# A Mamba layer on one core: GpSimd's operations in one written order, softplus by a timetable, a second DMA sum, and the residual added one chunk later

## The chip, the cores and the metric

The kernel runs on one core of a Trainium2 chip. The time is device microseconds (us) of one execution. Before the change, three runs took 2245.73, 2246.95 and 2251.04 us; the median is 2246.95 us. The engines have these short names in the profile: PE (TensorE, matrix products and transposes, which write to PSUM), ACT (ScalarE), DVE (VectorE), POOL (GpSimd) and SP (SyncE, which only issues DMAs here). Each works through its own queue in order. What a reader of one engine's result waits for is a semaphore.

## What is computed

The network has four layers; the change touches the first alone, two Mamba blocks m1 and m2 one behind the other on 2048 tokens (2 images of 1024 tokens) of 256 channels. Of the reference, cut to what matters:

```python
xs, res = jnp.split(u @ in_w + in_b, 2, axis=-1)       # 512 channels each
xs = silu(causal_conv4(xs) + conv_b)
dt, Bm, Cm = jnp.split(xs @ xproj_w, ...)               # 16 | 16 | 16
delta = softplus(dt @ dt_w + dt_b)
dA  = exp(delta[..., None] * A)                         # 16 states
dBu = delta[..., None] * Bm[:, :, None, :] * xs[..., None]
hst = dA_t * hst + dBu_t                                # over the tokens of an image
y_t = einsum('bdn,bn->bd', hst, C_t)
out = ((y + xs * Dp) * silu(res)) @ out_w + out_b       # then layer norm, and x is added
```

For each of the 16 states n there is a recurrence over the tokens for 512 channels, and y is a sum over n.

## The kernel before

**Units.** A block's tokens are cut into chunks of 512, so that there are eight units: m1's chunks 0 to 3, then m2's. `layer0` (from L662) lets three units overlap: while the scan of unit u runs, the back of unit u-1 (gate, silu, y, output projection, norm, residual) and the front of unit u+1 (convolution, x-projection, softplus) run in its gaps, and the entering projection of unit u+2.

**The scan of a unit** (`scan`, L461) goes over n = 0 to 15. For one n:
- POOL makes two products h = du * b of 128x1024 elements (L513). Their tile has six buffers, so POOL can lead by three n.
- ACT makes four decays da = exp(A delta) in PSUM (L525, three buffers).
- DVE runs four scans of 128x512 over them, in place in h (L529).
- PE transposes h in 16 pieces into PSUM tiles ht (L486, three buffers).
- The four tiles are weighted by C and summed into ya: by DVE, which adds in place (L501), or for some n by ACT, which only writes (L499).

ACT writes five of the 16 n: n = 0 into ya itself, n = 2 (`ASIDE`) into a second sum yb, and n = 4, 7 and 10 (`ADDED`) into a scratch tile `tail`, from which a DMA that POOL issues (L520) adds them into yb, `LATER` = 3 states on. At n = 3 of the next unit another such DMA adds yb into ya. yb and `tail` have one buffer each; ya has two.

**Softplus of the next unit** is done in two halves of 256 channels in `front`: PE's projection m_dt (L428), ACT's |.| and relu (L433, L437), exp (L440), ln (L442), then (e + 1) - 1 in two ACT steps on du (L448, L450), and on POOL sub, add, add to delta, and the product du = delta * x (L451, L453, L455, L457). Both halves use the same e and ln tiles.

**The back of a unit** (`back`) ends with the output projection into two PSUM tiles m_out_0 and m_out_2, the layer norm of their rows (`norm_rows`: statistics and `ln_off` on DVE, L176 to L184; `ln_rs` and the normalised rows `m_tail<-m_out` on ACT, L186), transposes back (mm_t, L197), ACT's scale and bias into `tail` (L627), and POOL's additions to x (L630; m2 adds its input x as well).

**PSUM.** The pool `ps_mm` (L674) has two buffers. The projections m_in, m_conv, m_dt, m_g, m_y, m_out and mm_t, and the tap products of layer 1 (w1t, taps_ps), all take their tiles from it.

**What sets the order.** The steps of these helpers are generators. `paced(63, steps)` spreads them over the 63 gaps ("slots") of a unit's scan: slot s comes after scan s + 1, so that n is about (s + 1) / 4. A tuple (g, many, first, end) gives `many` steps of g the slots from `first` up to `end`. That order of writing is only a priority: the framework's scheduler then decides, by dependences and free buffers, in which order each engine's instructions stand in its queue. The slots that matter here:

```python
            steps += [(f, Mamba.STEPS, 35, 63) for f in fronts]     # softplus, 18 steps
            steps += [(b, 4, 36, 50) for b in done]                 # output projection
            steps += [(e, Mamba.ENTER, 44, 62) for e in enters]     # entering projection
            steps += [(b, 3, 54, 62) for b in done]                 # norm, 2 x residual
```

A helper `behind` lets m2's diagonal tap matrices (POOL) follow the scan's products; for all else POOL's order is the scheduler's.

Of the kernel before, what the change touches and what calls it, by code (L numbers as in the profile page):

```python
# [66 lines left out]
class Net:  # L67


    def __init__(self, ctx, tc, cols, rows):  # L70
        self.tc, self.nc = tc, tc.nc
        nc = self.nc
        const = ctx.enter_context(tc.tile_pool(name="const", bufs=1))
        self.gates = []
# [82 lines left out]
    def functions(self, which, *after):  # L157

        with ExitStack() as order:
# [7 lines left out]
            )  # L167

    def norm_rows(self, outs, ins, by=None):

# [81 lines left out]
class Mamba:  # L252

    ASIDE = 2
    ADDED = 4, 7, 10
    LATER = 3
    ENTER = 4
    HEAD = 12  # L260
    STEPS = 18

    def __init__(self, net, m, pools, xt, x, in_w, out_w, xproj_w, dt_w):
        self.net, self.m, self.xt, self.x = net, m, xt, x
        self.wpool, self.one, self.two, self.scanp, self.dram, self.ps_mm, self.ps_da, self.ps_ht = pools
        self.weights = in_w, out_w, xproj_w, dt_w
        self.chunks = {}
        self.carry = None
        self.due, self.pre = {}, {}
# [19 lines left out]
    def diagonals(self):  # L289

        self.taps = self.wpool.tile(
            [P, NDC * 4, P], F32, tag="taps", name=f"{self.m}_taps"
        )
        for i in range(NDC * 4):
            self.net.nc.gpsimd.tensor_scalar_mul(
                self.taps[:, i, :], self.net.ident, self.net.col(f"{self.m}_conv_w", i)
            )
            yield

    def load_rest(self):  # L300
# [10 lines left out]
        for dc in range(NDC):  # L311
            nc.gpsimd.tensor_scalar_mul(self.skip[:, dc, :], net.ident, net.col(f"{m}_D", dc))
        yield
# [5 lines left out]
    def enter(self, j):  # L319

        net, nc, m, one = self.net, self.net.nc, self.m, self.one
        tok = slice(j * TC, (j + 1) * TC)
        pre = one.tile([P, NDC, 3 + TC], F32, tag="pre", name=f"{m}_pre_{j}")
        self.pre[j] = pre
        if self.first(j):
            nc.gpsimd.memset(pre[:, :, 0:3], 0.0)
        else:
            nc.gpsimd.tensor_copy(pre[:, :, 0:3], self.carry)
        for mc in range(NDC):
            ps = self.ps_mm.tile([P, TC], F32, tag="mm", name=f"{m}_in_{j}_{mc}")  # L330
            for kc in range(NCC):
                nc.tensor.matmul(  # L332
                    ps, lhsT=self.in_sb[:, kc, mc * P : (mc + 1) * P], rhs=self.xt[:, kc, tok],
                    start=(kc == 0), stop=(kc == NCC - 1),
                )
            nc.scalar.activation(pre[:, mc, 3:], ps, AF.Identity, bias=net.col(f"{m}_in_b", mc))
            if mc == NDC - 1 and not self.first(j + 1):
                self.carry = self.wpool.tile(
                    [P, NDC, 3], F32, tag="carry", name=f"{m}_carry_{j}", bufs=2
                )  # L340
                nc.gpsimd.tensor_copy(self.carry, pre[:, :, TC : TC + 3])
            yield

    def front(self, j, alone=False):
# [73 lines left out]
        else:  # L418
            parts = [slice(0, 2), slice(2, NDC)]
        for a in parts:  # L420
            if not alone:
                eb, lb = free[:, :2], free[:, 2:]
            else:
                eb, lb = e[:, a], ln[:, a]
            for k, dc in enumerate(range(a.start, a.stop)):
# [10 lines left out]
                else:  # L436
                    nc.scalar.activation(delta[:, dc, :], ps, AF.Relu, bias=b)  # L437
                yield
            with net.tc.issue_after(net.loaded.ins):
# [4 lines left out]
            w = du[:, a, :]  # L444
            if alone:
                nc.vector.tensor_scalar(w, eb, 1.0, -1.0, ALU.add, ALU.add)
            else:
                nc.scalar.activation(w, eb, AF.Identity, bias=net.one)  # L448
                yield
                nc.scalar.activation(w, w, AF.Identity, bias=net.minus_one)  # L450
            eng.tensor_sub(w, eb, w)  # L451
            yield
            eng.tensor_add(lb, lb, w)  # L453
            yield
            eng.tensor_add(delta[:, a, :], delta[:, a, :], lb)  # L455
            yield
            eng.tensor_mul(w, delta[:, a, :], xs[:, a, :])  # L457
            yield
        self.chunks[j] = xs, bd, ct, delta, du

    def scan(self, j, before, between, start=False, last=False):  # L461
# [18 lines left out]
        def rest(n, hs):  # L480


            for i in range(TPC):
# [23 lines left out]
        for n in range(NS):  # L507
# [3 lines left out]
            for g in range(NDC // G):  # L511
                h = scanp.tile(half, F32, tag="h", name=f"{m}_h_{j}_{n}_{g}", bufs=6)
                made = (nc.vector if start and n == 0 else nc.gpsimd).tensor_mul(  # L513
                    h, du[:, g * G : (g + 1) * G, :], b.unsqueeze(1).to_broadcast(half)
                )
                hs.append(h)
            self.product = made
# [20 lines left out]
        for _ in between:  # L538
            pass
        self.due = {} if last else {self.LATER: (ya, yb)}  # L540
        return before
# [5 lines left out]
    def back(self, j, last=False, joined=True):  # L547
# [24 lines left out]
        if last:  # L572
            tail = self.tail(f"{m}_tail_{j}")
            for cc in range(NCC):
                x = tail[:, (2 + cc) * TC : (3 + cc) * TC]
                at = j % (HW // TC) * TC
                nc.sync.dma_start(x, self.x[j // (HW // TC), cc, :, at : at + TC])
                nc.gpsimd.tensor_scalar_add(x, x, net.col(f"{m}_ln_b", cc))
                nc.gpsimd.tensor_add(xt[:, cc, tok], xt[:, cc, tok], x)
                yield  # L580
# [36 lines left out]
        for cc in range(NCC):  # L617
# [11 lines left out]
            )  # L629
            nc.gpsimd.tensor_add(xt[:, cc, tok], xt[:, cc, tok], r)  # L630
            if self.x is not None:
                x = tail[:, (3 - cc) * TC : (4 - cc) * TC]
                at = j % (HW // TC) * TC
                nc.sync.dma_start(x, self.x[j // (HW // TC), cc, :, at : at + TC])
                nc.gpsimd.tensor_add(xt[:, cc, tok], xt[:, cc, tok], x)
            yield
# [25 lines left out]
def layer0(net, x, x_dram, m1, m2, load_image, taps, conv_dram, lg):  # L662
# [5 lines left out]
    with (  # L668
# [27 lines left out]

        def behind(m, steps):

            while True:
                with tc.issue_after(m.product.ins):  # L700
                    if next(steps, steps) is steps:
                        return
                yield
# [5 lines left out]
        before, done = iter(()), []  # L709
        aside = taps.make(ps_mm, conv_dram)  # L710
        for u, (m, j) in enumerate(units):
            joined = u + 1 < len(units)
            steps = [(b, NDC, 4, 20) for b in done]
            if u:
# [16 lines left out]
            if u == NCH - 2:  # L731

                steps.append((behind(m, blocks[1].diagonals()), NDC * 4, 24, 40))
# [43 lines left out]
        for _ in islice(done[0], 2):  # L777
            pass
        acc = {2: taps.bank(ps_ht.tile([P, TC], F32, tag="ht", name="early_acc2"))}
        both(taps.convolve(0, pair, acc), done[0], 3)  # L780
# [1085 lines left out]
```

## Time and profile before

One execution was profiled. It took 2244.33 us, of which the trace spans 2242.6 us; the two differ by 1.7 us, and the median of the three runs is 2.6 us (0.12%) above it.

| what | us |
|---|---|
| profiled execution / its span | 2244.33 / 2242.6 |
| first scan starts | 51.7 |
| units 0 to 7, from first scan to first scan of the next | 107.3, 119.4, 138.7, 137.1, 138.4, 139.3, 146.2, 157 (to the last scan) |
| end of layer 0 | about 1169 |
| DVE busy in a unit 1 to 7 | 110.7 to 112.3 |
| mean granted clock of PE, whole span | 0.905 |

A page of the profile gives for a group of equal instructions the source line, the engine, out<-in by the names in the program, the count, the total and the mean time, and the idle time of that engine just ahead of them with what ended it. The waits are the same idle times sorted by who waited for whom ("us in total, times, longest us"). A timeline lists instructions with start and duration; in square brackets stands the idle time before one and what released it. A table of windows gives the busy time of each engine in stretches of the span, with the count of instructions, the granted PE clock, the share of DMA time and GB/s.

### The profile page before, as it was taken

To read this page: it belongs to the slowest core of one execution; us is meant where nothing else is said; L and a number is where in the kernel's file an instruction comes from. 1 tells how busy PE (TensorE), PEld (TensorE's weight loads), DVE (VectorE), ACT (ScalarE), POOL (GpSimd) and SP (SyncE) were. 2 spreads that over 40 slices of the span, in tenths; PEclk is the share of its full clock that TensorE was granted. 3 is DMA by queue.
4 is the path that set the end of the run, shared out by engine and by line. 5 is a ranking of instruction groups with operands and counts; after the bars stand their busy time and mean duration, and the time that the engine had idled before them with its cause. 6 is when DMAs were issued, how large, how long until landed. Compare 5 with 4: busy or idle time off the path is not lost.

```text
span 2242.6 us, 26709 instructions
## 1 busy us (share of the span) xinstructions
PE 1880.2 (84%) x9428; PEld 1306.9 (58%) x9428; DVE 1357.8 (61%) x2086; ACT 924.6 (41%) x1658; POOL 1042.8 (47%) x701
## 2 busy tenths in 40 slices
PE   7788778687787876879999989958999599949996
PEld 3454445444454553545565645637999467649994
DVE  6998959689696895978543285762222444442223
ACT  4777667566675665756321253321111122211111
POOL 3897679676786668875432350003333100023331
PEclk9889789797897978979999999978999799969997
DMA  2243323233232322442121000007999300059997
GB/s 104 67 106 78 78 72 75 66 76 81 70 93 58 87 63 56 103 91 67 30 47 20 29 33 0 19 19 267 329 330 337 138 1 20 17 180 320 332 326 284
DMA packets 94959, 256.33 MB, mean 114 GB/s; under 512 B 35963, under 2 KB 52224, under 8 KB 80228
## 3 DMA queue, kind: packets, MB, share of 16 engines
q1 hardware_dynamic: 77636, 198.29, 26.5%
q0 software_dynamic: 12192, 51.66, 9.8%
q10 hardware_dynamic: 4992, 4.59, 0.6%
q8 instruction: 79, 1.29, 0.3%
q14 instruction: 60, 0.49, 0.1%
HBM read 204.60 MB, written 19.37 MB: 100 GB/s over the span
## 4 chain that ended last, share of the span: by engine, by line
PE 32%; issue 6%; DVE 4%; DMA 4%; POOL 4%; ACT 1%; POOLq 0%; ACTq 0%; DVEq 0%
PE h L1673 6%; PE acc L883 3%; PE o L1687 3%; PE av L1397 3%; PE h L1220 2%; PE sc L1371 2%; DMA l_yd<-y,target 2%; POOL x L1643 2%; POOL l_yd L1693 2%; PE w L1229 1%; PE early_acc L883 1%; DMA x<-l_zd,source 1%; PE mm_t L197 1%; PE kvp L1129 1%; PE o L1042 1%
## 5 line engine op out<-in xcount | busy, mean ns | idle before, releaser
L513 POOL TENSOR_TENSOR m_h<-m_du,m_b 128x1024 f32<-128x1024 f32 x254 | 598.1, 2412 | 219.5 <-PE m_ht L486 95.7
L486 PE MATMUL m_ht<-ident,m_h 128*128 128x128 f32 x2048 | 369.4, 308 | 216.3 <-DVE m_ya L501 92.8
L486 PEld LDWEIGHTS m_ht<-ident,m_h 128*128 128x128 f32 x2048 | 263.3, 156 | 412.3 <-DVE m_h L529 145.8
L525 ACT ACTIVATE m_da<-m_delta,m_aneg 128x512 f32<-128x512 f32 x512 | 349.1, 691 | 254.3 <-DVE m_h L529 226.5
L529 DVE TENSOR_TENSOR_SCAN m_h<-m_da,m_state,m_h 128x512 f32<-128x512 f32 x256 | 316.7, 1267 | 70.9 <-POOL m_h L513 45.3
L1643 POOL DMA_INDIRECT x<-l_zd,source x82 | 84.0, 1025 | 578.1 <-issue 222.3
L529 DVE TENSOR_TENSOR_SCAN m_h<-m_da,m_h 128x512 f32<-128x512 f32 x256 | 301.0, 1205 | 69.7 <-POOL m_h L513 39.6
L1673 PEld LDWEIGHTS h<-xts,we 128*128 128x128 f32 x2528 | 297.3, 194 | 7.6 <-issue 3.9
L1673 PE MATMUL h<-xts,we 128*128 128x128 f32 x2528 | 298.5, 277 | 2.5 <-issue 1.9
L501 DVE SCALAR_TENSOR_TENSOR m_ya<-m_ht,m_ct,m_ya 128x512 f32<-128x512 f32 x352 | 253.0, 730 | 55.4 <-PE m_ht L486 54.8
L1679 ACT ACTIVATE hid<-h 128x512 f32<-128x512 f32 x79 | 47.2, 597 | 415.1 <-PE h L1673 415.1
L1680 DVE TENSOR_TENSOR hid<-hid,h 128x512 f32<-128x512 f32 x79 | 54.3, 687 | 266.6 <-PE h L1673 266.6
L1687 PE MATMUL o<-we,hid 128*128 128x256 f32 x632 | 150.6, 380 | 3.9 <-DVE hid L1680 2.3
L1693 POOL DMA_INDIRECT l_yd<-y,target x79 | 79.1, 1001 | 135.9 <-DVE y L1692 132.3
L367 PE MATMUL m_conv<-m_pre,m_taps 128*128 128x512 f32 x240 | 123.0, 639 | 1.4 <-ACT m_tail L627 1.1
L1687 PEld LDWEIGHTS o<-we,hid 128*128 128x128 f32 x632 | 113.7, 190 | 17.8 <-DVE hid L1680 3.0
L883 PE MATMUL early_acc<-x,early 128*98 128x448 f32 (+24 forms) x308 | 101.1, 455 | 0.4 <-DVE lg L900 0.4
L883 PE MATMUL acc<-x,pair 128*98 128x416 f32 (+21 forms) x308 | 92.8, 450 | 0.0
L332 PE MATMUL m_in<-x,m_in_sb 128*128 128x512 f32 x128 | 74.5, 715 | 2.6 <-DVE x L247 1.3
L1692 DVE COPY y<-o 128x256 f32<-128x256 f32 x79 | 33.5, 424 | 70.0 <-PE o L1687 69.8
L557 PE MATMUL m_g<-x,m_gate_sb 128*128 128x512 f32 x128 | 70.3, 664 | 5.1 <-ACT m_tail L186 4.5
L451 POOL TENSOR_TENSOR m_du<-m_e,m_du 128x1024 f32<-128x1024 f32 x14 | 33.2, 2372 | 83.8 <-ACT m_du L450 83.8
(319 smaller groups left out, 2787.1 us busy)
## 6 DMA issues: line engine op xcount, KB each, us to landing
we<-in_l_experts_dram SPq DMA_DIRECT2D x82, 1536.0 KB, 9.3
m_b<-m_bd SPq DMA_DIRECT2D x128, 256.0 KB, 3.3
m_yb<-m_s POOLq DMA_DIRECT2D x24, 1024.0 KB, 8.5
m_ya<-m_yb POOLq DMA_DIRECT2D x7, 1024.0 KB, 8.6
w<-in_l_w_dram SPq DMA_DIRECT2D x21, 256.0 KB, 2.7
l_zd<-l_z SPq DMA_DIRECT2D x7, 512.0 KB, 2.9
l_yl<-l_yd SPq DMA_DIRECT2D x10, 256.0 KB, 5.1
l_yl<-l_yd ACTq DMA_DIRECT2D x10, 256.0 KB, 5.9
```

The source lines that it names most:

```text
L332: nc.tensor.matmul(ps, lhsT=self.in_sb[:, kc, mc * P : (mc + 1) * P], rhs=self.xt[:, kc, tok], start=(kc == 0), stop=(kc == NCC - 1),)
L367: nc.tensor.matmul(ps, lhsT=self.taps[:, dc * 4 + k, :], rhs=pre[:, dc, k : k + TC], start=(k == 0), stop=(k == 3),)
L486: nc.tensor.transpose(ps[:, dc * P : (dc + 1) * P], hs[dc // G][:, dc % G, i * P : (i + 1) * P], net.ident,)
L501: nc.vector.scalar_tensor_tensor(ya[:, i, :], ps, c, ya[:, i, :], ALU.mult, ALU.add)
L513: made = (nc.vector if start and n == 0 else nc.gpsimd).tensor_mul(h, du[:, g * G : (g + 1) * G, :], b.unsqueeze(1).to_broadcast(half))
L525: net.decayed = nc.scalar.activation(da, delta[:, dc, :], AF.Exp, scale=self.aneg[:, i : i + 1])
L529: nc.vector.tensor_tensor_scan(h, da, h, 0.0 if first else state[:, n, dc : dc + 1], ALU.mult, ALU.add)
L883: nc.tensor.matmul(a[:, lo - 16 * k : hi - 16 * k, co : co + n], lhsT=lhsT, rhs=self.x[:, kc, b, lo - r0 : hi - r0, ci : ci + n], start=(u ...
L1643: nc.gpsimd.indirect_dma_start(out=x, out_offset=None, in_=zd[:, :], in_offset=bass.IndirectOffsetOnAxis(ap=source[:, g : g + 1], axis=0), ...
L1673: nc.tensor.matmul(ps[:, at], lhsT=w12[:, s, kc, at], rhs=xt[:, kc * P : (kc + 1) * P], start=(kc == 0), stop=(kc == NCC - 1),)
L1687: nc.tensor.matmul(ps[:, :C], lhsT=ht[:, mc * P : (mc + 1) * P], rhs=w[:, 8 + mc, :], start=(mc == 0), stop=(mc == NHC - 1),)
L1693: nc.gpsimd.indirect_dma_start(out=yd[g], out_offset=bass.IndirectOffsetOnAxis(ap=target[:, g : g + 1], axis=0), in_=y, in_offset=None, bo ...
```

## The change

1. **One order on POOL.** A new helper `lined` chains each operation that POOL gets in layer 0 (products, softplus, carry copies, residual, the summing DMAs, diagonals) behind the one written before it. `behind` goes; the chain is dropped for layer 0's last steps (`net.line = None`).
2. **Softplus by a timetable.** The 18 steps from slot 35 to 63 become seven groups with slots of their own: first half's projection and ACT steps at 33 to 41, its sub and add at 45 and 46, the second half's projection at 47 and 48, the first half's two last POOL steps at 49 and 50, the second half's ACT steps at 51 to 54, its sub and add at 57 and 58, its last two at 61 and 62.
3. **Second sum begun by a DMA.** `ASIDE` goes, `ADDED` becomes 2, 5, 8, 11: n = 2 also goes to `tail`, and its DMA writes yb instead of adding to it. ACT evicts five n as before; each unit has one DMA of 1 MB more. ACT no longer writes yb.
4. **Residual one chunk later.** Norm is one step at slot 59 (was 54), and the two residual steps of a back (`late`) move to slots 4 and 6 of the unit after; for the last unit they stay at its end.
5. **Smaller moves.** The entering projection is at slots 42 to 60 (was 44 to 62); the copy of its last three tokens (`carry`) moves to the start of the next `enter`.

PE, DVE, ACT and SP have the same number of instructions as before; POOL has eight DMA issues more.

```diff
-    ASIDE = 2
-    ADDED = 4, 7, 10
+    ADDED = 2, 5, 8, 11
-    STEPS = 18
+    STEPS = (6, 33, 41), (2, 45, 47), (2, 47, 49), (2, 49, 51), (4, 51, 55), (2, 57, 59), (2, 61, 63)
...
+    def lined(self, do, *args, **named):
+
+        with ExitStack() as order:
+            if self.line is not None:
+                order.enter_context(self.tc.issue_after(self.line.ins))
+            self.line = do(*args, **named)
...
+            (a, w), (b, v) = ((a, du[:, a, :]) for a in parts)
+            e, ln = free[:, :2], free[:, 2:]
+            yield from project(e, a)
+            yield from powers(e, ln, w)
+            first = sums(e, ln, w, a)
+            yield from islice(first, 2)
+            yield from project(e, b)
+            yield from first
+            yield from powers(e, ln, v)
+            yield from sums(e, ln, v, b)
...
-                to = {0: ya, self.ASIDE: yb}.get(n)
+                to = ya if n == 0 else None
...
-                        self.due[n + self.LATER] = yb, aside.rearrange("p (i d) -> p i d", d=DI)
+                        self.due[n + self.LATER] = (
+                            yb, aside.rearrange("p (i d) -> p i d", d=DI), n != self.ADDED[0]
+                        )
...
-                made = (nc.vector if start and n == 0 else nc.gpsimd).tensor_mul(
-                    h, du[:, g * G : (g + 1) * G, :], b.unsqueeze(1).to_broadcast(half)
-                )
+                factors = du[:, g * G : (g + 1) * G, :], b.unsqueeze(1).to_broadcast(half)
+                if start and n == 0:
+                    nc.vector.tensor_mul(h, *factors)
+                else:
+                    net.lined(nc.gpsimd.tensor_mul, h, *factors)
...
             if n in self.due:
-                with net.tc.issue_after(made.ins):
-                    nc.gpsimd.dma_start(*self.due.pop(n), accum_op=ALU.add)
+                to, a, add = self.due.pop(n)
+                op = ALU.add if add else ALU.bypass
+                net.lined(nc.gpsimd.dma_start, to, a, accum_op=op)
...
-            nc.gpsimd.tensor_add(xt[:, cc, tok], xt[:, cc, tok], r)
+            net.lined(nc.gpsimd.tensor_add, xt[:, cc, tok], xt[:, cc, tok], r)
...
+            ready = done
+            if joined:
+                done = [islice(b, 2 * NDC + 5) for b in done]
...
-            steps += [(f, Mamba.STEPS, 35, 63) for f in fronts]
+            for n, first, end in Mamba.STEPS:
+                steps += [(f, n, first, end) for f in fronts]
             steps += [(b, 4, 36, 50) for b in done]
-            steps += [(e, Mamba.ENTER, 44, 62) for e in enters]
-            steps += [(b, 3, 54, 62) for b in done]
+            steps += [(e, Mamba.ENTER, 42, 60) for e in enters]
+            steps += [(b, 2, 4, 8) for b in late]
+            steps += [(b, 1, 59, 60) for b in done]
+            if u + 1 == len(units):
+                steps += [(b, 2, 61, 63) for b in done]
+            late = ready
```

More of the change, by code (lines that the diff above doesn't have):

```diff
@@ L73, in __init__ @@
         const = ctx.enter_context(tc.tile_pool(name="const", bufs=1))
-        self.gates = []
+        self.gates, self.line = [], None
         self.small = ctx.enter_context(tc.tile_pool(name="small", bufs=4))
@@ L267, in __init__ @@
         self.chunks = {}
-        self.carry = None
         self.due, self.pre = {}, {}
@@ L294, in diagonals @@
         for i in range(NDC * 4):
-            self.net.nc.gpsimd.tensor_scalar_mul(
-                self.taps[:, i, :], self.net.ident, self.net.col(f"{self.m}_conv_w", i)
+            self.net.lined(
+                self.net.nc.gpsimd.tensor_scalar_mul, self.taps[:, i, :], self.net.ident, self.net.col(f"{self.m}_conv_w", i)
             )
@@ L311, in load_rest @@
         for dc in range(NDC):
-            nc.gpsimd.tensor_scalar_mul(self.skip[:, dc, :], net.ident, net.col(f"{m}_D", dc))
+            net.lined(
+                nc.gpsimd.tensor_scalar_mul, self.skip[:, dc, :], net.ident, net.col(f"{m}_D", dc)
+            )
         yield
@@ L322, in enter @@
         tok = slice(j * TC, (j + 1) * TC)
-        pre = one.tile([P, NDC, 3 + TC], F32, tag="pre", name=f"{m}_pre_{j}")
+        if not self.first(j):
+            carry = self.wpool.tile([P, NDC, 3], F32, tag="carry", name=f"{m}_carry_{j}", bufs=2)
+            net.lined(nc.gpsimd.tensor_copy, carry, self.entered[:, :, TC : TC + 3])
+        self.entered = pre = one.tile([P, NDC, 3 + TC], F32, tag="pre", name=f"{m}_pre_{j}")
         self.pre[j] = pre
         if self.first(j):
-            nc.gpsimd.memset(pre[:, :, 0:3], 0.0)
+            net.lined(nc.gpsimd.memset, pre[:, :, 0:3], 0.0)
         else:
-            nc.gpsimd.tensor_copy(pre[:, :, 0:3], self.carry)
+            net.lined(nc.gpsimd.tensor_copy, pre[:, :, 0:3], carry)
         for mc in range(NDC):
@@ L336, in enter @@
             nc.scalar.activation(pre[:, mc, 3:], ps, AF.Identity, bias=net.col(f"{m}_in_b", mc))
-            if mc == NDC - 1 and not self.first(j + 1):
-                self.carry = self.wpool.tile(
-                    [P, NDC, 3], F32, tag="carry", name=f"{m}_carry_{j}", bufs=2
-                )
-                nc.gpsimd.tensor_copy(self.carry, pre[:, :, TC : TC + 3])
             yield
@@ L419, in front, with project @@
             parts = [slice(0, 2), slice(2, NDC)]
[L420 to L424, printed above, removed]
+        def project(eb, a):
             for k, dc in enumerate(range(a.start, a.stop)):
@@ L438, in front, with powers @@
                 yield
+        def powers(eb, lb, w):
             with net.tc.issue_after(net.loaded.ins):
@@ L443, in front @@
             yield
-            w = du[:, a, :]
             if alone:
@@ L450, in front, with sums @@
                 nc.scalar.activation(w, w, AF.Identity, bias=net.minus_one)
-            eng.tensor_sub(w, eb, w)
             yield
[L453 to L458, printed above, removed]
+        def sums(eb, lb, w, a):
+            d = delta[:, a, :]
+            for out, x, y, add in (
+                (w, eb, w, eng.tensor_sub), (lb, lb, w, eng.tensor_add),
+                (d, d, lb, eng.tensor_add), (w, d, xs[:, a, :], eng.tensor_mul),
+            ):
+                if alone:
+                    add(out, x, y)
+                else:
+                    net.lined(add, out, x, y)
+                yield
+        if alone:
+            for a in parts:
+                w = du[:, a, :]
+                yield from project(e[:, a], a)
+                yield from powers(e[:, a], ln[:, a], w)
+                yield from sums(e[:, a], ln[:, a], w, a)
+        else:
+            (a, w), (b, v) = ((a, du[:, a, :]) for a in parts)
[8 more added lines that the diff above has]
+            yield from sums(e, ln, v, b)
         self.chunks[j] = xs, bd, ct, delta, du
@@ L495, in rest @@
                         aside = self.tail(f"{m}_s_{j}_{n}")[:, : TPC * DI]
-                        self.due[n + self.LATER] = yb, aside.rearrange("p (i d) -> p i d", d=DI)
+                        self.due[n + self.LATER] = (
+                            yb, aside.rearrange("p (i d) -> p i d", d=DI), n != self.ADDED[0]
+                        )
                     to = self.due[n + self.LATER][1]
@@ L512, in scan @@
                 h = scanp.tile(half, F32, tag="h", name=f"{m}_h_{j}_{n}_{g}", bufs=6)
-                made = (nc.vector if start and n == 0 else nc.gpsimd).tensor_mul(
-                    h, du[:, g * G : (g + 1) * G, :], b.unsqueeze(1).to_broadcast(half)
-                )
+                factors = du[:, g * G : (g + 1) * G, :], b.unsqueeze(1).to_broadcast(half)
+                if start and n == 0:
+                    nc.vector.tensor_mul(h, *factors)
+                else:
+                    net.lined(nc.gpsimd.tensor_mul, h, *factors)
                 hs.append(h)
-            self.product = made
             if n in self.due:
-                with net.tc.issue_after(made.ins):
-                    nc.gpsimd.dma_start(*self.due.pop(n), accum_op=ALU.add)
+                to, a, add = self.due.pop(n)
+                op = ALU.add if add else ALU.bypass
+                net.lined(nc.gpsimd.dma_start, to, a, accum_op=op)
             for dc in range(NDC):
@@ L539, in scan @@
             pass
-        self.due = {} if last else {self.LATER: (ya, yb)}
+        self.due = {} if last else {self.LATER: (ya, yb, True)}
         return before
@@ L577, in back @@
                 nc.sync.dma_start(x, self.x[j // (HW // TC), cc, :, at : at + TC])
-                nc.gpsimd.tensor_scalar_add(x, x, net.col(f"{m}_ln_b", cc))
-                nc.gpsimd.tensor_add(xt[:, cc, tok], xt[:, cc, tok], x)
+                net.lined(nc.gpsimd.tensor_scalar_add, x, x, net.col(f"{m}_ln_b", cc))
+                net.lined(nc.gpsimd.tensor_add, xt[:, cc, tok], xt[:, cc, tok], x)
                 yield
@@ L634, in back @@
                 nc.sync.dma_start(x, self.x[j // (HW // TC), cc, :, at : at + TC])
-                nc.gpsimd.tensor_add(xt[:, cc, tok], xt[:, cc, tok], x)
+                net.lined(nc.gpsimd.tensor_add, xt[:, cc, tok], xt[:, cc, tok], x)
             yield
@@ L695, in layer0 @@
         norm.image(0)
[L697 to L703, printed above, removed]
         units = [(m, j) for m in blocks for j in range(NCH)]
@@ L708, in layer0 @@
             pass
-        before, done = iter(()), []
+        before, done, late = iter(()), [], []
         aside = taps.make(ps_mm, conv_dram)
@@ L731, in layer0 @@
             if u == NCH - 2:
-                steps.append((behind(m, blocks[1].diagonals()), NDC * 4, 24, 40))
+                steps.append((blocks[1].diagonals(), NDC * 4, 24, 40))
             rest = m.load_rest() if u and j == 0 else iter(())
             steps += [(rest, 1, 37, 38)]
-            steps += [(f, Mamba.STEPS, 35, 63) for f in fronts]
+            for n, first, end in Mamba.STEPS:
+                steps += [(f, n, first, end) for f in fronts]
             steps += [(b, 4, 36, 50) for b in done]
-            steps += [(e, Mamba.ENTER, 44, 62) for e in enters]
-            steps += [(b, 3, 54, 62) for b in done]
+            steps += [(e, Mamba.ENTER, 42, 60) for e in enters]
[4 more added lines that the diff above has]
+            late = ready
             steps += [(rest, 1, 62, 63)]
@@ L778, in layer0 @@
             pass
+        net.line = None
         acc = {2: taps.bank(ps_ht.tile([P, TC], F32, tag="ht", name="early_acc2"))}
```

## The prediction

> **What bounds the kernel now.** I took the busy shares first, then the table of windows by unit, the waits of the first 1150 us, and the timelines of POOL, ACT and DVE around one change of unit.
>
> Over the whole span PE is the busiest:
>
> ```profile
> PE 1880.2 (84%) x9428; PEld 1306.9 (58%) x9428; DVE 1357.8 (61%) x2086; ACT 924.6 (41%) x1658; POOL 1042.8 (47%) x701
> ```
>
> The change touches layer 0 alone, the first 1169 us. Its windows, one for a unit (start:end, length, busy us of PE, PEld, DVE, ACT, POOL):
>
> ```profile
> 159.00:278.40 119.40, 93.86 (x415) 56.44 (x416) 111.67 (x124) 77.81 (x120) 87.50 (x42) 0.89 0.31 77
> 278.40:417.10 138.70, 107.69 (x476) 65.91 (x475) 110.76 (x124) 91.14 (x169) 107.95 (x63) 0.85 0.31 76
> ```
>
> DVE is the bound here: busy for about 111 us in each unit, idle 7.7 in unit 1, but 27.9, 26.0, 27.5, 27.0 and 35.0 in units 2 to 6. What it and its neighbours wait for:
>
> ```profile
> POOL m_h L513 <- PE m_ht L486: 95.7, 26, 14.2
> DVE m_h L529 <- POOL m_h L513: 84.8, 11, 14.4
> POOL m_du L451 <- ACT m_du L450: 83.8, 7, 17.2
> DVE m_h L529 <- ACT m_da L525: 55.5, 24, 6.5
> ACT m_yb L499 <- DMA m_ya<-m_yb: 45.6, 7, 8.5
> ```
>
> Lines two and three are one chain: seven waits of POOL, one for each change of unit, and behind them DVE. From POOL's timeline, unit 1 to 2:
>
> ```profile
> 267.23 2.36 POOL L513 TENSOR_TENSOR m_h<-m_du,m_b 128x1024 f32<-128x1024 f32 x1 [2.82 <-issue]
> 286.63 2.35 POOL L451 TENSOR_TENSOR m_du<-m_e,m_du 128x1024 f32<-128x1024 f32 x1 [17.05 <-ACT m_du L450]
> 288.94 1.26 POOL L630 TENSOR_TENSOR x<-x,m_tail 128x512 f32<-128x512 f32 x1
> ...
> 296.10 2.34 POOL L457 TENSOR_TENSOR m_du<-m_delta,m_xs 128x1024 f32<-128x1024 f32 x1
> 298.52 13.89 POOL L513 TENSOR_TENSOR m_h<-m_du,m_b 128x1024 f32<-128x1024 f32 x6
> ```
>
> DVE's, same place:
>
> ```profile
> 285.69 0.75 DVE L501 SCALAR_TENSOR_TENSOR m_ya<-m_ht,m_ct,m_ya 128x512 f32<-128x512 f32 x1 [0.34 <-PE m_ht L486]
> 300.89 5.84 DVE L529 TENSOR_TENSOR_SCAN m_h<-m_da,m_h 128x512 f32<-128x512 f32 x5 [14.45 <-POOL m_h L513]
> ```
>
> POOL has made n = 0's first product, stands 17.05 us until ACT has the second half's (e + 1) - 1, works through four softplus steps and two residual additions, and only then makes n = 0's second product; DVE loses 14.45. And ACT's, where the delay begins:
>
> ```profile
> 267.64 0.57 ACT L186 ACTIVATE m_tail<-m_out,ln_off,ln_rs 128x256 f32<-128x256 f32 x1
> ...
> 276.35 0.69 ACT L433 ACTIVATE m_e<-m_dt,cols_sb 128x512 f32<-128x512 f32 x1 [0.81 <-PE m_dt L428]
> ```
>
> The second half's projection follows the norm's reads of m_out (end 268.2). Where no back runs, at the change 0 to 1, it stands at 132.16, 20 us ahead of the end of n = 14; at the six others it always comes after the norm, by 8.15, 5.5, 6.9, 7.5, 8.6 and 1.35 us. I read that as the two buffers of `ps_mm`: m_out_0 and m_out_2 hold both until the norm has read them.
>
> **Part 1: order and timetable.** The timetable writes the second projection at slot 47, but m_out takes its buffers at 36 and 43 and now gives them back at 59 instead of 54. In the changed program's queues PE accordingly still has m_dt_2 behind the norm; ACT's second half comes no earlier. What does move is POOL: its queue now reads ..h_14, DMA, sub, add, h_15, h_15, delta, mul, h_0, h_0, h_1, h_1, residual, h_2.. Behind the waiting sub are queued the two products of n = 15, for which DVE's scans wait. Times from the end of n = 14's last scan (269.37 here) by rows:
>
> - DVE accumulates two tiles and finishes statistics and ln_off (0.64 a step): +4.25. Norm reads 1.91 as before (266.29 to 268.20): +6.2.
> - To the projection's first ACT step two tap copies, as at 6 to 7 (1.35): 1.65, +7.85. Then up to the end of (e + 1) - 1, before 276.35 to 286.55 = 10.2, less one decay and a state copy that no longer stand between: 9.35, +17.2. Before: 286.55 - 269.37 = 17.2. **The wait ends when it did.**
> - sub, add, product, 2.35 each: n = 15's first scan at +24.4, DVE idle about 19.6. Four scans: +29.3. POOL: product, delta, mul, product: +33.7, n = 0 starts at +33.9 (gap 4); n = 1 ends at +45.3. Residual after it (below), h_2 at +48.75 (gap 2), n = 3 ends at +59.6.
>
> Before, n = 3 ended at +56.97, 55.42, 57.25, 56.73 (changes 1 to 2 up to 4 to 5), 60.71 (5 to 6), 48.72 (6 to 7). For m2's four additions I get +60.9 at 5 to 6; at 6 to 7, where ACT was already early, +55.5.
>
> **Part 2: what leaves the path.** ln_off, four elements wide, is stretched while POOL makes products:
>
> ```profile
> L180 DVE TENSOR_TENSOR ln_off<-zeros,ln_mv 128x4 f32<-128x4 f32 x7 | 21.7, 3105 | 0.0
> ```
>
> It took 2.99, 5.03, 3.14, 3.93, 2.99 and 3.49 in units 1 to 6, and 0.16 where POOL stood. At slot 59 POOL stands at its sub, so 2.9, 4.9, 3.0, 3.8, 2.85 and 3.35 go, ahead of the +0. So after - before: 1 to 2: 59.6 - 56.97 - 2.9 = -0.3; then -0.7, -0.65, -0.9, -2.65, and 55.5 - 48.72 - 3.35 = +3.45. At 0 to 1 only ACT's wait for yb goes; it held DVE for 3 to 5 us, some of which other work (silu, n = 3's products) takes back: -2.8. Sum **-4.5**. The other six yb waits lie within n = 3 and are in the sums above.
>
> **Part 3: DMAs and evictions.** Eight issues more, 862 ns each by POOL's row of m_yb<-m_s, are 6.9 us. They fall at n = 5, where POOL waits for PE (first line of the waits, 95.7): 0, at most +6.9 if that cover were gone. n = 4's ACT evictions leave the crowded stretch around silu (n = 6 takes about 11 us against 6 to 7), n = 5's first comes into it and must wait for n = 2's DMA to leave the one `tail` (8.5 us median). Rows on both sides: -2 (three evictions of 0.68) to +1; nearer to the first I take -0.6, six times: **-4**.
>
> **Part 4: end, residual, carry.** In unit 7, n = 11's DMA goes out one n later than n = 10's did: the norm waits till about 1105 instead of 1098.4, but the gates then run together, and PE is full there anyway (139.5 of 156.9 us): 0, between -4 and +4. Residual: two (m2: four) additions of 1.26 leave the chain ahead of n = 0 and stand ahead of h_2, counted above. Carry copies of 0.19 us, chained: 0; uncovered, 16 times 0.2 = +3.
>
> **Sum** against the profiled execution: 2244.33 - 4.5 - 4 = 2236. The median lies 2.6 above that execution, 0.12%; 0.3%, about 6.7 us, is what a measurement of this kernel can tell from no change.
>
> One rule speaks against this change: the Trainium skill, "Perfetto Trace Analysis", section Optimization Strategy, says that the same gap repeating on the engine that should be saturated can mean too little SBUF or PSUM for the next tile. The seven like waits fit it; by it the gap stays at about 17 us, and by a timetable that alone decided the order the time would be rival 1's. No run here has another buffer count.
>
> **Rivals.**
> 1. *The bubble goes as written* (the second half is ready by n = 15). n = 0 of units 2 to 6 takes 24.8, 24.6, 26.2, 25.4, 27.3 us, against 7.3 in unit 1: 128.3 - 36.5 = -92; ln_off -21; yb -3 at each change, -20. About 2112 to 2150. For it: at 0 to 1 exactly this happens. Against: PE's queue. 7%.
> 2. *Slower: the stretch from the norm to the projection is as long as before.* I took 1.65; five rows say 5.5 to 8.6, because taps, entering projection and m_dt take the two buffers in turn. Each us is a us of the DVE gap. At +4 to +7 for five changes (20 to 35): 2256 to 2271. It turns the sign from (4.5 + 4) / 6 = 1.4 us a change on, and is measurable from 2.5. For it: five of six rows; against: in the new queue only tap work stands between. 28%.
> 3. *A wash*: n = 5's eviction waits its full landing between two silu steps (+3 for each unit instead of -0.6), or the end costs 4. 2238 to 2251. 25%.
>
> **How the numbers follow.** Forecast, the bubble moved ahead of n = 15 and a small gain left: 40%, 2222 to 2238, likeliest 2236. Faster by over 0.3%: 40 + 7 = 47%; within: 25%; slower: 28%. The range takes in forecast, wash and most of rival 2; it leaves out rival 1 and the ends: 2212 to 2266. Both signs hold much of the chance; the forecast's own range is 2222 to 2238.
>
> **What would show it.** Right: POOL's wait for ACT's du is still 80 us or more but stands ahead of n = 15's products; DVE idle of 17 to 21 us ahead of n = 15's first scan, 4 ahead of n = 0's, 2 ahead of n = 2's; ACT's wait for the yb DMA gone; ln_off at 0.2 us; n = 0 down to about 10 us, n = 15 up. Wrong: m_dt ahead of the norm on PE (rival 1), or more than 9 us from the norm to it (rival 2), or ln_off still stretched because POOL isn't standing.

## The result, and the profile after

The changed kernel takes 2284.93 us (median of four runs, 2282.33 to 2290.81) against 2248.99 us for the kernel before in the same rounds: a ratio of 1.0164, 95% interval 1.0137 to 1.019. It is slower, where the forecast was 2236 us and its range ended at 2266. The profiled execution took 2286.4 us, its span is 2284.7 us: 42.1 us more than the span before.

From the page, busy time over the whole span:

```profile
PE 1936.5 (85%) x9428; PEld 1327.6 (58%) x9428; DVE 1336.9 (59%) x2086; ACT 932.1 (41%) x1658; POOL 1046.2 (46%) x709
```

DVE is busy for 21 us less than before, which is the stretched `ln_off` (L180 before, L187 here); its group's line:

```profile
L187 DVE TENSOR_TENSOR ln_off<-zeros,ln_mv 128x4 f32<-128x4 f32 x7 | 1.1, 151 | 0.0
```

The waits in the first 1150 us (us in total, times, longest):

```profile
POOL m_du L174 <- ACT m_du L453: 175.2, 8, 30.6
DVE m_h L559 <- POOL m_h L174: 170.3, 23, 27.1
DVE m_h L559 <- ACT m_da L555: 23.2, 28, 4.4
DVE ln_st L183 <- PE m_out L636: 14.2, 6, 3.4
```

POOL's wait for ACT's du step has doubled, 83.8 to 175.2, and so has DVE's for POOL, 84.8 to 170.3. ACT's wait for the yb DMA (45.6) is gone, and a new one is there: DVE's layer-norm statistics wait for the output projection in the middle of a unit. (All of POOL's chained operations carry line 174, that of `lined`.)

POOL's timeline at the change from unit 1 to 2:

```profile
263.30 2.35 POOL L174 TENSOR_TENSOR m_h<-m_du,m_b 128x1024 f32<-128x1024 f32 x1
265.58 0.82 POOL L174 DMA_DIRECT2D m_yb<-m_s  x1
296.20 2.34 POOL L174 TENSOR_TENSOR m_du<-m_e,m_du 128x1024 f32<-128x1024 f32 x1 [29.79 <-ACT m_du L453]
298.61 2.35 POOL L174 TENSOR_TENSOR m_e<-m_e,m_du 128x1024 f32<-128x1024 f32 x1
300.92 4.64 POOL L174 TENSOR_TENSOR m_h<-m_du,m_b 128x1024 f32<-128x1024 f32 x2
```

DVE's at the same place:

```profile
277.47 0.74 DVE L529 SCALAR_TENSOR_TENSOR m_ya<-m_ht,m_ct,m_ya 128x512 f32<-128x512 f32 x1
303.29 4.81 DVE L559 TENSOR_TENSOR_SCAN m_h<-m_da,m_state,m_h 128x512 f32<-128x512 f32 x4 [25.08 <-POOL m_h L174]
312.62 2.34 DVE L559 TENSOR_TENSOR_SCAN m_h<-m_da,m_h 128x512 f32<-128x512 f32 x2 [4.52 <-POOL m_h L174]
```

And ACT's:

```profile
277.59 1.93 ACT L193 ACTIVATE m_tail<-m_out,ln_off,ln_rs 128x256 f32<-128x256 f32 x4 [0.90 <-DVE ln_off L191]
...
283.19 0.69 ACT L435 ACTIVATE m_e<-m_dt,cols_sb 128x512 f32<-128x512 f32 x1 [1.72 <-PE m_dt L430]
...
287.92 0.69 ACT L435 ACTIVATE m_e<-m_dt,cols_sb 128x512 f32<-128x512 f32 x1 [0.39 <-PE m_dt L430]
...
294.95 1.15 ACT L453 ACTIVATE m_du<-m_du,minus_one 128x1024 f32<-128x1024 f32 x1
```

The picture is the one forecast: the second projection behind the norm, POOL standing at the sub, n = 15 behind it. But the gap is 25.1 us, not 19.6, and too little has been won elsewhere to pay for it.

Where the 42.1 us lie, by the same marks in both traces (T0 is the end of n = 14's last scan; "du" below is ACT's (e + 1) - 1 on the second half, the step that POOL's sub waits for):

| stretch | before | after | difference |
|---|---|---|---|
| start to T0 of unit 0 | 152.0 | 158.4 | +6.4 |
| seven stretches from T0 to the end of the next unit's n = 3 | 371.3 | 419.8 | +48.5 |
| six stretches from there to the next T0 | 489.4 | 481.3 | -8.1 |
| from n = 3 of unit 7 to the end | 1229.9 | 1225.2 | -4.7 |

### The profile page after: what moved, and what is told of

Same layout as the page of the kernel before. It is cut to its first block, busy times and chain, and to the rows that moved or that the text cites. A ratio compares the mean times of both kernels' runs of the same rounds, so it can differ in the third digit from the quotient of the medians.

```text
span 2284.7 us, 26736 instructions
## 1 busy us (share of the span) xinstructions
PE 1936.5 (85%) x9428; PEld 1327.6 (58%) x9428; DVE 1336.9 (59%) x2086; ACT 932.1 (41%) x1658; POOL 1046.2 (46%) x709
## 3 DMA queue, kind: packets, MB, share of 16 engines
q0 software_dynamic: 13344, 60.05, 10.6%
## 4 chain that ended last, share of the span: by engine, by line
PE 31%; issue 6%; DMA 4%; DVE 4%; POOL 4%; ACT 1%; POOLq 0%; SPq 0%; ACTq 0%; DVEq 0%
PE h L1704 6%; PE acc L914 3%; PE o L1718 3%; PE av L1428 2%; PE h L1251 2%; PE sc L1402 2%; DMA l_yd<-y,target 2%; POOL x L1674 2%; POOL l_yd L1724 1%; PE w L1260 1%; PE early_acc L914 1%; DMA l_yl<-l_yd 1%; DMA x<-l_zd,source 1%; PE mm_t L204 1%; PE kvp L1160 1%
## 5 line engine op out<-in xcount | busy, mean ns | idle before, releaser
L512 PE MATMUL m_ht<-ident,m_h 128*128 128x128 f32 x2048 | 383.1, 314 | 187.8 <-DVE m_ya L529 100.2
L512 PEld LDWEIGHTS m_ht<-ident,m_h 128*128 128x128 f32 x2048 | 268.4, 158 | 410.8 <-DVE m_h L559 138.3
L174 POOL TENSOR_TENSOR m_du<-m_e,m_du 128x1024 f32<-128x1024 f32 x14 | 34.5, 2466 | 175.2 <-ACT m_du L453 175.2
L527 ACT ACTIVATE m_s<-m_ht,m_ct 128x512 f32<-128x512 f32 x128 | 85.7, 681 | 15.9 <-PE m_ht L512 14.5
L342 PE MATMUL m_in<-x,m_in_sb 128*128 128x512 f32 x128 | 84.4, 795 | 3.8 <-ACT m_delta L439 2.1
```

The lines of the kernel that those rows point to most:

```text
L174: self.line = do(*args, **named)
L512: nc.tensor.transpose(ps[:, dc * P : (dc + 1) * P], hs[dc // G][:, dc % G, i * P : (i + 1) * P], net.ident,)
L527: nc.scalar.activation(to[:, i, :], ps, AF.Copy, scale=c)
```

## The experiments

Each time is a median, each ratio is to the kernel before in the same rounds, with its 95% interval. The kernels whose names begin with a are edits of the changed kernel, those with b of the kernel before.

### Do the two PSUM buffers hold the second half back?

Both kernels got the same edit of one line: the second half's two m_dt tiles from the pool of the transposes.

```diff
-pool, tag = (self.ps_ht, "ht") if alone and dc else (self.ps_mm, "mm")
+pool, tag = (self.ps_ht, "ht") if dc > (0 if alone else 1) else (self.ps_mm, "mm")
```

**a_dt_ht.** 

> The changed kernel, with the second half's two m_dt tiles taken from the pool of the transposes (three buffers) instead of ps_mm. Theory (banks): what holds the second half is that m_out keeps both ps_mm buffers until the norm; freed of that, softplus follows its timetable, POOL's wait for du falls from 175 us to under 30, the 25 us gap ahead of n = 15 goes at five changes of unit and 16 at the sixth, and the time is 2100 to 2160 us. Rival (the written POOL order or ACT's amount of work is what costs): the gap stays, 2270 to 2300 us.

Measured: 2181.73 us, ratio 0.9707 (0.9678 to 0.9736): 103 us faster than the changed kernel. Its waits:

```profile
POOL x L174 <- ACT m_tail L657: 81.8, 12, 14.8
...
POOL m_du L174 <- ACT m_du L453: 7.5, 8, 2.3
```

The wait for du is gone, 175.2 to 7.5, as the buffer theory said; n = 15 and the end of n = 14 are short. The time is 22 us above the expected range, and the first line names a reason: at each change of unit POOL now stands at the residual additions, which in the written order come ahead of n = 2's products. From its POOL timeline, unit 1 to 2:

```profile
301.04 1.27 POOL L174 TENSOR_TENSOR x<-x,m_tail 128x512 f32<-128x512 f32 x1 [11.92 <-ACT m_tail L657]
303.66 1.27 POOL L174 TENSOR_TENSOR x<-x,m_tail 128x512 f32<-128x512 f32 x1 [1.35 <-ACT m_tail L657]
304.88 9.28 POOL L174 TENSOR_TENSOR m_h<-m_du,m_b 128x1024 f32<-128x1024 f32 x4
```

**b_dt_ht.** 

> The kernel before, with the same edit of one line (m_dt tiles of the second half from the transposes' pool). Banks: n = 0 of units 2 to 6 falls from 25 us to about 8, time 2140 to 2180 us. Rival (the scheduler's free order is what makes the bubble there, not the buffers): 2235 us or more.

Measured: 2162.22 us, ratio 0.9621 (0.9594 to 0.9648). n = 0 of units 2 to 6 fell from 24.6 to 27.3 us to 6.2 to 8.0, and DVE's wait for POOL's products from 84.8 us to this:

```profile
DVE m_h L529 <- POOL m_h L513: 34.4, 24, 5.7
```

So the two buffers made the gap in both kernels, and neither the order on POOL nor a timetable is needed to remove it.

### The change in parts

**b_added**: part 3 alone (`ADDED` 2, 5, 8, 11, yb begun by a DMA) in the kernel before.

> The kernel before with part 3 alone: n = 2, 5, 8 and 11 into the scratch tile, yb written by DMA only. Expected: ACT's wait for the yb DMA (45.6 us) goes, n = 3 of units 1 to 7 falls from 9 to 12 us to about 7, n = 6 by about 3; time 2220 to 2238 us. Rival (DVE has other waits there at once, or one scratch tile makes n = 5 wait): 2240 to 2255 us.

Measured: 2230.46 us, 0.9922 (0.9895 to 0.995). n = 3 falls to 5.1 to 5.4 us. But unit 0 takes 113.8 us instead of 107.3 (n = 6 9.8 for 7.9, n = 10 10.6 for 7.1), and T0 of unit 0 comes 5.7 us later: most of the +6.4 of the changed kernel there comes with this part.

**a_unlined**: the changed kernel, POOL's order left to the scheduler.

```diff
-            if self.line is not None:
+            if self.line is not None and do == self.nc.gpsimd.dma_start:
```

> The changed kernel without the written order on POOL (only the DMA sums stay behind the operation ahead of them); all else as changed. If the place of the waiting sub in POOL's queue, ahead of n = 15's products, is the loss, the time falls back to about 2240 to 2255 us. If the loss is that the chain after the norm is longer (more work of PE and ACT between norm and du), wherever the sub stands, it stays at 2270 to 2300 us, with the gap of DVE at n = 0 instead of n = 15.

Measured: 2263.92 us, 1.0073 (1.0051 to 1.0095): between the two. DVE's gap is at n = 0 again, now 30 to 36 us for that n, and du ends 25.6 to 30.7 us after T0 at the changes 1 to 2 up to 5 to 6, later even than with the written order. So about 21 us are the written order's, and not all of the loss.

**a_unlined_steps18**: also without the timetable, `STEPS = (20, 35, 63),`.

> The changed kernel without the written order and without the timetable: what is left over b_added (2230 us) is the norm at slot 59 and the residual one chunk later. If the late norm is the loss: 2255 us or more, as a_unlined (2264). If the timetable was the loss in a_unlined: 2228 to 2240 us.

Measured: 2249.65 us, 1.0015 (0.9999 to 1.0032): between the two expectations. Read as a ladder: 0.9922 with the second sum alone; 1.0015 with the norm at slot 59, the late residual and the earlier entering projection; 1.0073 with the timetable; 1.0164 with the written order. The second sum gains 0.8%, and each of the three others costs, 0.9%, 0.6% and 0.9%. These shares hold for this order of steps alone: a_steps18 below takes the timetable out with the order kept, and gains nothing.

### Four single edits within the changed kernel

**a_norm54**: the norm step back at slot 54.

```diff
-            steps += [(b, 1, 59, 60) for b in done]
+            steps += [(b, 1, 54, 55) for b in done]
```

> The changed kernel with the norm step back at slot 54 (was 59 in the change); residual stays late. If the late norm is what makes the second half late (the buffers come free about 7 us later), the end of ACT's du step moves from 23 to 24 us after the last scan of n = 14 back to 15 to 18, DVE's gap ahead of n = 15 falls from 25 to about 19 us, and the time is 2240 to 2258 us. Rival (the chain between norm and du is longer for other reasons): 2270 us or more.

Measured: 2278.47 us, 1.0151 (1.0109 to 1.0193). That is the second expectation: the interval overlaps that of the changed kernel. Yet du did come earlier, 17.7 to 19.8 us after T0 at four changes (23.2 at the fifth), and with it DVE's first scan of n = 15, at 24.9 to 26.9 us (30.4 at the fifth) instead of 30.0 to 31.7; sub, add and a product of 2.35 us each still stand between the two. The seven stretches from T0 to n = 3 fell from 419.8 to 401.1 us, and the six between them took half of that back (490.3 instead of 481.3). Part of it is the norm, which now waits 28.7 us in all for the DMA of n = 11's tile. So the late norm costs at the change of unit, and moving it back costs elsewhere.

**a_sub_late**: the second half's sub and add behind n = 15's products.

```diff
-(2, 57, 59), (2, 61, 63)
+(2, 60, 62), (2, 62, 63)
```

> The changed kernel with the second half's sub and add at slots 60 and 61 and its last two steps at 62, so that the written POOL order has n = 15's products ahead of the waiting sub; norm stays at 59. If the place in POOL's queue costs, DVE works through n = 15 while ACT catches up: 2255 to 2272 us. If it costs nothing, because the work of n = 15 only delays the norm and the projection as much: 2280 to 2292 us.

Measured: 2280.96 us, 1.0151 (1.0115 to 1.0188): the second expectation. DVE works through n = 15 at once, but at five changes the norm's reads then start 6.5 to 7.5 us after T0 instead of 3.9 to 4.7, du ends at +22.5 to +29.5 (+22.8 to +24.5 in the changed kernel), and the gap comes at n = 0. The place of the sub ahead of n = 15 is not what costs.

**a_steps18**: the timetable undone, the order kept. (The changed kernel's softplus has 20 steps, not 18, since each half's sub is now a step of its own.)

> The changed kernel with the softplus timetable undone (its 20 steps evenly from slot 35 to 63), written order kept. If the timetable costs, because it puts ACT's and POOL's first half into n = 9 to 12 and sub and add ahead of n = 15's products: 2255 to 2275 us. If the order alone is the loss: 2280 to 2300 us.

Measured: 2288.83 us, 1.0181 (1.0144 to 1.0218): the second expectation. Within the written order the timetable is no loss.

**a_early_res**: the residual additions at slots 61 and 62 of the same unit.

> The changed kernel with the residual additions back at the end of the same unit (slots 61 and 62, within the written order) instead of slots 4 and 6 of the next. If late residual is a gain: the additions, which wait for ACT's tail, hold the products of n = 0, 2290 to 2305 us. If it is a loss (gap of 1 to 3 us ahead of n = 2 goes): 2270 to 2282 us.

Measured: 2289.15 us, 1.0177 (1.0139 to 1.0215): between the two expectations, and not clear of the changed kernel. n = 1 of units 2 to 6 falls from 7.5 to 10.3 us to 5.0 to 5.4, n = 15 of units 1 to 6 rises from 9.3 to 11.7 us to 11.7 to 14.4: the additions are paid wherever they stand in the order.

### The residual once the gap has gone

**a_dt_ht_res**: a_dt_ht with the residual additions out of the written order (plain `nc.gpsimd.tensor_add` in the last loop of `back`).

> The changed kernel with m_dt in the transposes' pool and the residual additions of all units but the last out of the written POOL order, at the same slots. In a_dt_ht n = 1 takes 17 to 20 us, and POOL waits 82 us for ACT's m_tail ahead of the additions. If the written order makes that loss (products of n = 2 queue behind the additions), n = 1 falls to 6 to 8 us and the time to 2105 to 2130 us. Rival (the tail itself is late and the products wait for something else): 2160 us or more.

Measured: 2166.15 us, 0.9653 (0.9607 to 0.9699). n = 1 of units 2 to 6 fell from 17 to 20 us to 5 to 7, as the first theory said, but n = 2 and n = 3 took some of it back (6.4 to 11.3 us, against 5.2 to 5.6 in a_dt_ht), so that the gain over a_dt_ht is 16 us and not the 50 or more expected. By the time it is the rival's case, by n = 1 the first theory's.

### The clock in the stretch from norm to du

The forecast gave 11.0 us to the stretch from the end of the norm's reads to the end of du (1.65 + 9.35). At five changes of the changed kernel it took 16.6, 16.6, 15.8, 18.6 and 17.1. PE is busy for 91 to 98% of it. The granted clock is the share of its full clock at which PE was let run. Windows of 2 us in the changed kernel (start:end, length, busy PE, PEld, DVE, ACT, POOL, then the granted PE clock):

```profile
279.00:281.00 2.00, 2.00 (x10) 1.66 (x9) 0.00 (x0) 0.84 (x3) 0.00 (x0) 0.50 0.00 0
...
285.00:287.00 2.00, 2.00 (x4) 0.50 (x3) 0.00 (x0) 0.16 (x1) 0.00 (x0) 0.54 0.00 0
287.00:289.00 2.00, 1.46 (x6) 0.57 (x5) 0.00 (x0) 1.61 (x3) 0.00 (x0) 1.00 0.00 0
...
291.00:293.00 2.00, 1.92 (x6) 0.88 (x4) 0.00 (x0) 1.24 (x3) 0.00 (x0) 0.50 0.00 0
```

Before, at the same change:

```profile
272.00:273.00 1.00, 1.00 (x2) 0.23 (x1) 1.00 (x1) 0.00 (x0) 0.00 (x0) 0.50 0.00 0
...
274.00:275.00 1.00, 1.00 (x13) 1.00 (x10) 0.95 (x2) 0.95 (x3) 0.00 (x0) 1.00 0.32 39
```

Before, the full clock is granted from 274 on, ahead of the second projection at 275.19, whose two matmuls took 1.12 us and m_in's four 1.98. In the changed kernel the two m_dt matmuls at 281.02 took 2.07 us and m_in's four 3.78: the same work at half the clock.

**a_warm** keeps PE busy ahead of the norm. Nothing reads the added transposes; the real ones overwrite them.

```diff
+                for dc in range(NDC if n in (12, 13, 14) and not last else 0):
+                    nc.tensor.transpose(ps[:, dc * P : (dc + 1) * P], net.ident, net.ident)
```

> The changed kernel with PE kept busy ahead of the norm: in n = 12, 13 and 14 of units 0 to 6 each transpose tile is first filled with four transposes of the identity that nothing reads (48 a unit more of 128x128, overwritten by the real ones). In the changed kernel the granted clock stands at 0.50 to 0.65 from 270 to 288 us, where m_dt and m_in take twice their time. If the clock makes the chain from norm to du longer than forecast (23 to 24 us against 17), it shrinks by 3 to 5 us at each change and the time falls to 2255 to 2272 us, with a clock near 1.0 in that stretch. Rival (the chain is ACT's work and waits for buffers, the clock only accompanies it): 2280 us or more.

Measured: 2280.07 us, 1.0144 (1.0108 to 1.018). The clock had fallen back by the time of the projection at most changes; only at 2 to 3 did it stay up (0.87), and there the stretch fell from 16.6 to 13.0. Inconclusive, so:

**a_warm2**: as a_warm, but with eight such transposes a tile in n = 14, and four ahead of each m_dt of the second half.

> As a_warm, with more idle work for PE: eight unread transposes of the identity a tile in n = 14, and four ahead of each of the second half's m_dt products (2 tiles a unit). In a_warm the clock of the stretch from norm to du rose at one change only (0.64 to 0.87 at 2 to 3, where the stretch fell from 16.6 to 13.0 us) and at the others the stretch fell by 0.1 to 2.5. If the clock is what makes PE's work in that stretch long: the stretch is 12 to 14 us wherever its mean clock is 0.85 or more, at most changes, and the time is 2258 to 2274 us. If it is not: the stretch stays at 15 to 17 us at a raised clock, or grows by the added work, 2278 us or more.

Measured: 2271.67 us, 1.0124 (1.0097 to 1.015). The stretch is now 14.4, 13.1, 12.5, 13.8 and 14.4 at clocks of 0.88, 1.00, 1.00, 1.00 and 0.88. The stretch at the change 3 to 4 in three kernels, before first:

```profile
546.60:563.70 17.10, 17.10 (x80) 10.54 (x80) 13.31 (x16) 13.73 (x24) 0.41 (x1) 0.89 0.17 46
```

the changed kernel:

```profile
574.30:590.10 15.80, 14.79 (x40) 6.64 (x39) 0.00 (x0) 9.81 (x14) 0.00 (x0) 0.70 0.14 40
```

a_warm2:

```profile
560.30:572.80 12.50, 11.12 (x47) 6.04 (x45) 0.00 (x0) 9.59 (x14) 0.00 (x0) 1.00 0.19 51
```

Before, PE did 80 matmuls in the stretch, 30 of them transposes of n = 14 and n = 15. In the changed kernel those of n = 14 are done ahead of it and those of n = 15 wait behind the sub, so half as many matmuls are left, yet the stretch is barely shorter; with the clock held up, and more matmuls, it is 3.3 us shorter. The mean over the five changes falls from 16.9 to 13.6, which is 16.4 us in all; the median time fell by 13. The 95% intervals of the two times overlap, but each of the four runs is faster than each of the four of the changed kernel. The stretch of a_warm2 holds two groups of the added transposes, 0.60 and 0.63 us at the change 3 to 4, each just ahead of an m_dt product, so that the clock's own part is likely more than 3.3 us.

### The second sum once the gap has gone

**b_dt_ht_added**: b_dt_ht and b_added together.

> The kernel before with two edits that each gained alone: the second half's m_dt tiles in the transposes' pool (2162 us) and the DMA-begun second sum (2230 against 2248, -17.5). If the two are independent: 2140 to 2150 us. If the yb wait had lost its weight once the bubble is gone (27.5 us of waits are left in that profile instead of 45.6): 2152 to 2163 us.

Measured: 2161.03 us, 0.9627 (0.9591 to 0.9663): no gain over b_dt_ht. A wait that this profile has and that of b_dt_ht has not:

```profile
ACT m_tail L186 <- DMA m_yb<-m_s: 31.4, 5, 10.7
```

n = 11's DMA leaves one n later than n = 10's did, and the norm needs the same tile.

**b_dt_ht_added1**: the same with `ADDED = 1, 4, 7, 10`, so that the last DMA leaves when it did before.

> The kernel before with m_dt of the second half in the transposes' pool, and the DMA-begun sum with n = 1, 4, 7, 10 instead of 2, 5, 8, 11, so that the last DMA leaves at n = 13 as before the change. b_dt_ht_added (2161) gained nothing over b_dt_ht (2162): its norm waits 31 us for the DMA of n = 11's tile, which has one buffer. If that wait ate the gain: 2138 to 2152 us. If the yb wait was worth nothing once the bubble had gone: 2157 us or more.

Measured: 2144.84 us, 0.955 (0.9526 to 0.9575), the fastest version here, 101 us under the kernel before and 140 under the changed one. From its page:

```profile
PE 1859.5 (87%) x9428; PEld 1304.5 (61%) x9428; DVE 1375.3 (64%) x2086; ACT 922.7 (43%) x1658; POOL 1049.7 (49%) x709
```

DVE's idle time in units 1 to 6 is 3.6 to 9.8 us each. The longest n left there is n = 14 (12.7 to 15.1 us), where `ln_off` still meets POOL's products (5.4 to 6.9 us each).

## Why the prediction was wrong

**What holds the second half: right, shown.** PE's queue, the seven like waits, and the change 0 to 1, where no back runs, were read as the two buffers of `ps_mm`; another pool for two tiles removed the gap in both kernels. The page of the Trainium skill that was weighed ("Perfetto Trace Analysis", Optimization Strategy) names too few buffers as a possible cause of such a gap. Here it was the cause: -86 us in the kernel before (2248.0 to 2162.2), close to the -92 that rival 1 put on it.

**The bubble moves ahead of n = 15: right in place.** At five changes the norm's reads start 3.9 to 4.7 us after T0 (4.25 forecast), n = 0's gap is 3.2 to 5.1 (4), and from the end of du to the end of n = 3 it takes 41.5 to 43.4 us (59.6 - 17.2 = 42.4). At 6 to 7 n = 3 ends at +56.7 (55.5).

**"The wait ends when it did": the step that failed.** The prediction let du end at +17.2, as before: 1.65 us from the norm's end to the first ACT step of the second half, and 9.35 from there to the end of du. Measured at five changes: 2.7 to 4.1, and 12.9 to 15.0; du ends at +22.8 to +24.5. The 9.35 came from ACT's timeline at a place where PE ran at full clock, with transposes of n = 14 and n = 15 among its work; the change that was being priced takes just those out of the stretch, and there the mean clock is 0.63 to 0.70. The 1.65 came from the change 6 to 7, the only one at which the changed kernel took no longer (0.3). The 5.6 to 7.3 us that this cost at each of five changes are rival 2's case (4 to 7, from 1.4 on slower), given 28%. Rival 2 named waits for the two buffers as its cause; a_warm2 shows the clock as at least half of it (16.9 to 13.6 us of the stretch), and the 2.6 us that stay above 11.0, the added transposes among them, were not split further. Summed over all changes, the stretches from T0 to n = 3 are 32 us longer than forecast (419.8 against 387.5).

**What leaves the path: right at `ln_off`, wrong in the middle.** `ln_off` takes 0.15 us each, as forecast, and units 1 to 6 together take 78.5 us from n = 13 to T0 instead of 107.9, where 20.8 were taken off. But n = 4 to 12 grew from 381.9 to 403.0, where 4 were taken off. n = 6, which part 3 was priced by, did fall, by 1.3 to 2.9 us a unit; but the n that ACT writes have moved, and n = 4, 5 and 8 gave more than that back (n = 4 to 8: 219.9 before, 226.2 after, 227.8 in b_added). The rest lies at n = 9, which grew by 23.4 us while n = 10 to 12 fell by 8.7: DVE's queue has the first of the norm's statistics there, ahead of scans, and they wait for the output projection (14.2 us in six waits); ACT's softplus steps delay decays there as well (9.9 us). The traces of the experiments show which edit moved the statistics. The first two of a back stand at n = 11 in the kernel before, at n = 10 with part 3 alone (b_added) and with the timetable undone (a_steps18, a_unlined_steps18), and the first at n = 9 wherever the timetable is in; with `ADDED = 1, 4, 7, 10` in the kernel before they stay at n = 11. The prediction had looked at DVE's queue only from n = 14 on.

**Unit 0: missed.** Part 3 was costed by its gain at later units; in unit 0, which has no back and no yb wait, T0 comes 6.4 us later (5.7 in b_added).

**The end: near.** -4.7 us, forecast 0 between -4 and +4.

The failed stretch (32), the middle (17) and unit 0 (6), less 5 at the end, make up the 51 us between -8.5 and +42.1. The range ended at 2266 because it took rival 2 with all other terms at their forecast; two of those were off in the same direction.

**What stays open.** How the 21 us of the written order divide between n = 0's products, which without it are made ahead of the sub, and the additions; the runs show only that n = 15's place is not it (a_sub_late), and that the additions cost most once the gap has gone (a_dt_ht_res).

## What to carry to other kernels

When a stage is late, ask which buffer its first instruction takes and who gives that buffer back last; no order of issue moves it ahead of that. A duration taken from a place where other work kept an engine warm does not hold where the change removes that work. A written order on an in-order engine makes each wait in it everybody's wait: put in it only what is ready by then, and look through the whole unit of each neighbour's queue, not the place of the change alone.

## What the runs showed of the hardware

**The clock.** The granted PE clock stood at 0.50 where PE was idle for about a quarter of the time or more (busy 5.35 of 7 us from 270 to 277 in the changed kernel, 3.12 of 7 from 258 to 265 in the kernel before). At these places it rose to 1.00 only after about 8.2 us of unbroken work in the changed kernel (busy from 278.7, full clock from 286.8), about 7.5 in the kernel before (from 266.4, full from 273.9). It fell back to 0.50 at 290.2, after 3.4 us with PE busy for 2.63 of them. The Trainium skill, "TensorE: Matmul & The Clock Gate", section Part 1, gives one busy window of about 3.4 us as the condition; the free-running windows it describes would allow up to two of them, 6.8 us, by an estimate from that page, less than either of the two measured. The record of the granted clock in these two traces has only the values 0.50 and 1.00, and all its changes lie whole multiples of 3.41 us apart. All 36 rises of the kernel before and all 47 of the changed kernel come at the end of such a step with PE busy for 80% of it or more. But not each busy step brings a rise: from 267.05 to 270.47 in the kernel before and from 279.99 to 283.41 in the changed kernel PE was busy throughout, and the clock rose one step later. What sets those steps apart stays open.

**`ln_off` beside POOL.** Each of the six `ln_off` that met POOL's products in the kernel before ended 0.03 to 0.04 us after the end of a product, the second or third to end since `ln_off` had started: it did not get its turn after the product that was running. POOL's next product began 2.82 to 2.84 us after that end; the profile puts three of these waits to nothing and three to ACT's reads of the norm. In b_dt_ht_added1 it is 5.35 to 6.93 us for `ln_off`, through three or four operations of POOL, and 2.68 to 2.76 us of standing behind it, all six put to nothing. Why POOL stands then was not tested.
